# Second layer of a two-layer graph-attention kernel: denominators spread by small DMAs, both context halves transposed in one run, side results read a key tile later

## The chip, the cores and the metric

The kernel runs on one core of one Trainium2 chip. A core has five engines that work side by side, each through its own instructions in program order: TensorE (PE, matmul; PEld is its weight load), VectorE (DVE), ScalarE (ACT), GpSimd (POOL) and SyncE (SP, which here issues DMAs). The metric is the device time of one launch in microseconds (us), lower is better.

## What is computed

Two layers over 8 graphs of 2048 nodes with 256 features. The first layer is attention by chunks of keys under an adjacency mask, with a projection and a layer norm; the change does not touch it. The second layer, the one that matters here, is a graph attention with 4 heads of 64 features:

```python
h = relu(layernorm(x));  q = (h @ W).reshape(B, N, H, D)
e = e_src[:, :, None, :] + e_dst[:, None, :, :]
e = where(e >= 0, e, 0.2 * e);  e = where(adj > 0, e, -9e15)
h_prime = einsum('bijh,bjhd->bihd', softmax(e, axis=2), q)
x = x + elu(h_prime.reshape(B, N, H * D))
```

The kernel uses that exp of a leaky sum of two terms is the larger of two products, so a tile of the weights is one DVE instruction: the maximum of a row (`near`) and a per-key number (`far`), cut by the mask (`limit`). The softmax's denominators are summed beside the numerators and divided out at the end.

## The kernel before, in words

All of the second layer stands in `layers`, and its instruction order is written out by hand: what is recorded first on an engine runs first there.

**Passes and tiles.** There are 32 passes, one for each graph b and head h (`passes`), and each walks over 16 key tiles jt = 0..15 of 128 keys. The loop over `rounds` records for tile jt, in this order:

- `begun` for the tile two ahead: DVE makes `e` (L804, 128 x 2048; in tiles 0 and 15 as two halves). `e` has five buffers (`second_e`), so e of tile n + 5 can only be written when every reader of e of tile n is done. At tile 14 `begun` also records `nears` of the next pass (L795): ACT rewrites the one `near` buffer, after the last e of this pass has read it, and the next e waits for ACT.
- `weigh_rows` (L815): 8 matmuls of 32 x 512 into the two context banks `acc`, as 16 instructions.
- for the denominators, tiles are added in pairs m = 0..7 (tiles 2m, 2m + 1). On the even tile ACT scales e into `t` (L926, two halves); on the odd tile POOL adds the second e to it (L932, two halves). The sums of a pair are due two tiles after its odd tile (L826, into the bank `rest[:, 0]`, called `den`). Pairs 3 and 7 (`SINGLE`) go to PE without ACT and POOL.
- at tile 15, ACT copies the two banks `acc` to `cT` (L939) and `den` to `dT` (L948), and a generator `ending(k, cT, dT)` is put first in the list `aside`.
- `advance()` takes one step of the generators in `aside`. A step that ends with a bare `yield` has used the one side bank `rest[:, 1]` (`aux()`) and ends the call; one that ends with `yield True` lets the next generator have its step too.

**The end of a pass** (`ending`) is spread over the next pass's first tiles. Step by step: the load of `xh` (L842, SP; at tile 15); tile 0: four transposes (`flip`, L157) of `dT`, then the reciprocal and a maximum on DVE (L848, L849); tiles 1 and 2: four transposes of one context half each, and on DVE the product with the inverse denominators, `z` (L858); tiles 3 and 5: four ACT instructions for one half of the elu (L870 to L873); tiles 4 and 6: two POOL additions for that half (L875, L876); tile 7: the output DMA (L878, SP).

**The preparation of the next graph** (`preparation`, started in the first pass of every four, except for the last graph) shares the side bank. For four blocks of rows: ACT makes `h` (L145), PE transposes (`turn`, L157), ACT copies to `hT` (L165), twice, then 8 small matmuls (L622) and an ACT copy. Then reductions, two DMA hops, and a transpose of `er`. Then eight times: `sides` (L154, 32 instructions of 128*32 x 256) and the DVE product `qn` (L693) that reads its bank. A graph's four passes with a preparation in them are called a group below; there are seven groups, and then four plain passes (28 to 31) without one.

The functions that the change touches, with their callers:

## Time and profile before

| what | us |
|---|---|
| median of 3 runs (lowest, highest) | 4203.39 (4202.0, 4207.51) |
| the profiled execution's own time | 4210.55 |
| its span | 4208.7 |
| first instruction of L815 (second layer) | 2730.5 |
| last pass's `cT` copies begin | 4188.6 |
| mean granted TensorE clock | 0.994 |
| busy: PE / DVE / ACT / POOL | 4067.2 / 3159.1 / 2394.9 / 3263.0 |

The page gives shares over the whole span, and over two thirds of that is the first layer. The second layer's passes repeat: from pass 4 on, each group takes 183.6 us between the same copies of its passes, and each of the passes 28 to 30 takes 40.43 us. So one plain pass and one group are read in the timelines, and the rest is counted. An engine's idle time before an instruction, and what ended it, stand in brackets at the end of its line; "DVE e L804" there means that DVE's instruction of line 804 ended the wait.

### The profile page before, as it was taken

Reading aid. Unit: us, or ns where it says so; the run is one execution under the profiler, and the core shown is the slowest. Engines: PE = TensorE matmul, PEld = TensorE weight load, DVE = VectorE, ACT = ScalarE, POOL = GpSimd, SP = SyncE. Lnnn points to the kernel's source line nnn. Section 1 sums busy time; section 2 is a strip of 40 time slices with the busy share of each in tenths; the row PEclk is TensorE's granted clock in tenths of the full one; section 3 lists DMA queues with packets and bytes.
Section 4 is the critical chain, followed back from the end, with each engine's and each line's share of the span. In section 5 each row is a group of like instructions: output and inputs, shape, how many; then the busy total and the mean of one; then the engine's idle time right before and its main releaser. Section 6 shows DMA issues by size and latency. Waiting matters only on the chain. (4 is left out here: it accounts for less than half of the span.)

```text
span 4208.7 us, 85702 instructions
## 1 busy us (share of the span) xinstructions
PE 4067.2 (97%) x34998; PEld 1507.0 (36%) x34998; DVE 3159.1 (75%) x3526; ACT 2394.9 (57%) x3090; POOL 3263.0 (78%) x1735
## 2 busy tenths in 40 slices
PE   7999999999999999999999999889999999999998
PEld 3333333333333333333333333333333333333333
DVE  5786676666766677676677677588888988888897
ACT  5655565555565565555556556564555646555554
POOL 2577787888888888788788799777776877777687
PEclk9999999999999999999999999999999999999999
DMA  3221211112112112111211222221221222122121
GB/s 112 87 77 50 57 58 48 53 53 65 48 55 63 48 51 61 54 50 53 62 50 54 55 60 62 80 58 51 63 71 33 72 52 73 51 63 71 33 61 37
DMA packets 343235, 248.11 MB, mean 59 GB/s; under 512 B 225840, under 2 KB 293168, under 8 KB 342832
## 3 DMA queue, kind: packets, MB, share of 16 engines
q1 hardware_dynamic: 337648, 223.66, 19.6%
q0 software_dynamic: 5184, 18.88, 1.2%
q8 instruction: 277, 4.54, 0.4%
q14 instruction: 126, 1.03, 0.1%
HBM read 204.15 MB, written 36.18 MB: 57 GB/s over the span
## 5 line engine op out<-in xcount | busy, mean ns | idle before, releaser
L449 DVE SCALAR_TENSOR_TENSOR E<-big,limit 128x1024 f32<-128x1024 f32 x1024 | 1181.9, 1217 | 646.1 <-PE big L441 627.9
L742 POOL TENSOR_TENSOR add<-E 128x1024 f32<-128x1024 f32 x512 | 1203.7, 2374 | 496.1 <-PE both L461 472.7
L455 ACT ACTIVATE E<-E 128x1024 f32<-128x1024 f32 x1024 | 1055.7, 1057 | 687.8 <-DVE E L449 669.1
L804 DVE SCALAR_TENSOR_TENSOR e<-near,far,limit 128x2048 f32<-128x2048 f32 (+1 forms) x576 | 1183.0, 2107 | 94.3 <-issue 55.0
L932 POOL TENSOR_TENSOR t<-t,e 128x1024 f32<-128x1024 f32 x384 | 903.9, 2383 | 346.4 <-ACT t L926 196.0
L461 PE MATMUL both<-E,v 128*32 128x512 f32 x8192 | 993.9, 594 | 0.2
L815 PE MATMUL acc<-e,qn 128*32 128x512 f32 x8192 | 972.8, 595 | 5.3 <-DVE e L804 5.1
L441 PE MATMUL big<-qT,kT 64*128 64x512 f32 x4096 | 959.4, 606 | 14.6 <-DVE E L449 12.5
L441 PEld LDWEIGHTS big<-qT,kT 64*128 64x128 f32 x4096 | 366.2, 187 | 587.7 <-issue 419.8
L926 ACT ACTIVATE t<-e,quot 128x1024 f32<-128x1024 f32 x384 | 420.1, 1144 | 266.5 <-DVE e L804 153.1
L501 POOL TENSOR_TENSOR acc<-acc,c 128x1024 f32<-128x1024 f32 x224 | 531.2, 2371 | 4.6 <-DVE c L499 4.6
L461 PEld LDWEIGHTS both<-E,v 128*32 128x32 f32 x8192 | 294.3, 109 | 535.8 <-issue 396.7
L815 PEld LDWEIGHTS acc<-e,qn 128*32 128x32 f32 x8192 | 271.8, 110 | 496.0 <-issue 451.4
L499 DVE TENSOR_TENSOR c<-both,r 128x512 f32<-128x512 f32 x448 | 308.7, 690 | 42.3 <-PE both L461 10.6
L472 PE MATMUL big<-add,ones 128*32 128x512 f32 x2048 | 280.7, 601 | 13.9 <-POOL add L742 3.4
L826 PE MATMUL rest<-t,for_sums 128*32 128x512 f32 x1536 | 211.0, 594 | 22.2 <-DVE z L858 9.5
L479 ACT COPY s<-big 128x512 f32<-128x512 f32 x256 | 149.8, 585 | 71.1 <-PE big L472 70.8
L826 PE MATMUL rest<-e,for_sums 128*32 128x512 f32 x1024 | 141.0, 592 | 0.0
L145 ACT ACTIVATE h<-x,off,rstd 128x256 f32<-128x256 f32 x256 | 139.2, 593 | 0.0
L154 PE MATMUL rest<-w,hT 128*32 128x256 f32 x1952 | 122.1, 392 | 10.7 <-DVE qn L693 6.6
L795 ACT ACTIVATE near<-es,off_s 128x1024 f32<-128x1024 f32 x64 | 71.6, 1119 | 106.8 <-DVE e L804 95.8
L154 PE MATMUL big<-hT,wk 128*32 128x512 f32 x1024 | 124.2, 600 | 7.0 <-ACT hT L165 5.8
(133 smaller groups left out, 3031.3 us busy)
## 6 DMA issues: line engine op xcount, KB each, us to landing
r<-inv SPq DMA_DIRECT2D x1024, 64.0 KB
x<-in_x_dram SPq DMA_DIRECT2D x96, 512.0 KB
es<-er SPq DMA_DIRECT2D x64, 512.0 KB
adj_in<-in_adj_dram SPq DMA_DIRECT2D x32, 512.0 KB
x<-o POOLq DMA_DIRECT2D x32, 512.0 KB, 3.3
xh<-x SPq DMA_DIRECT2D x32, 512.0 KB
out_dram<-xh SPq DMA_DIRECT2D x32, 512.0 KB
x<-x SPq DMA_DIRECT2D x28, 512.0 KB
```

The lines of the kernel that those rows point to most:

```text
L441: nc.tensor.matmul(ps[:, hh, :], ks[kt // NT][own, hp, (kt % NT) * P : (kt % NT + 1) * P], qs[qb][own, hp, :], start=True, stop=True,)
L449: nc.vector.scalar_tensor_tensor(e, ps, -0.5, bcast(limit[:, qb, kt, :], 1, 2), ALU.max, ALU.min)
L455: nc.scalar.activation(e, e, AF.Exp, scale=0.25 * EDGE)
L461: nc.tensor.matmul(both[part][32 * h : 32 * h + 32, :], vs[kt // NT][:, kt % NT, mine], es[h // 2][:, h % 2, :], start=first, stop=not first,)
L499: nc.vector.tensor_tensor(to[:, part, :], both[part], r, ALU.mult)
L501: nc.gpsimd.tensor_tensor(acc, acc, to, ALU.add)
L742: nc.gpsimd.tensor_tensor(both, tiles[0][hp], tiles[1][hp], ALU.add)
L804: nc.vector.scalar_tensor_tensor(e[:, of, :], near[:, of, :], far[:, jt, h : h + 1], limit[:, of, jt, :], ALU.max, ALU.min,)
L815: nc.tensor.matmul(acc[part][32 * blk : 32 * blk + 32, :], qn[jt // NT][:, jt % NT, own], e[:, blk, :], start=(jt == 0), stop=(jt == NKT - 1),
L826: nc.tensor.matmul(den[32 * blk : 32 * blk + 32, :], for_sums[:, jt, :], blocks[blk], start=first, stop=last,)
L926: nc.scalar.activation(t, now[:, 2 * half : 2 * half + 2, :], AF.Copy, scale=quot[:, m, h : h + 1])
L932: nc.gpsimd.tensor_tensor(ts[half], ts[half], now[:, 2 * half : 2 * half + 2, :], ALU.add)
```

## The change

Only the second layer is changed.

- In `ending`, the four transposes of `dT` go. In their place SP issues four DMAs that spread the four rows of denominators over 128 partitions (16 bytes to each partition from each row); then the load of `xh` as four DMAs in place of one. Rows are now dealt to partitions as (block, partition, tile), so `cT` is copied from `acc` with a stride of four.
- Both context halves are transposed in one run of eight, into the side bank and into `den`'s bank, and the reciprocal, the maximum and both products follow each other on DVE.
- A list `unread` holds readers of side results. `aux()` and `advance()` call them first, so these are recorded one key tile later: the ACT copy to `hT`, the DVE products `qn`, and the reciprocal, maximum and products of the ending.
- With three steps fewer on the side bank, ending's later steps come two tiles earlier (elu halves on ACT at tiles 1 and 3, on POOL at tiles 2 and 4, output at tile 5), and so do the preparation's steps.
- The output goes out in four DMAs.

```diff
+    def read_all():
+        while unread:
+            unread.pop(0)()
+    def read_later(reader):
+        if rest:
+            unread.append(reader)
+        else:
+            reader()
     def aux(dtype=F32):
+        read_all()
         return rest[0][:, 1, :] if rest else pair(dtype)[:, 0, :]
...
-        nc.scalar.copy(
-            hT[:, :, two * 256 : (two + 1) * 256].rearrange("p c (t r) -> p c t r", t=2), ps
-        )
+        to = hT[:, :, two * 256 : (two + 1) * 256].rearrange("p c (t r) -> p c t r", t=2)
+        read_later(lambda: nc.scalar.copy(to, ps))
...
     def advance(all_of=True, mask_first=False):
+        read_all()
         moved = all_of and tick()
...
-                nc.vector.tensor_tensor(
-                    q[:, 2 * two : 2 * two + 2, :].rearrange("p t (h d) -> p (t h) d", h=H),
+                read_later(lambda to=q[:, 2 * two : 2 * two + 2, :], ps=ps, n=n: nc.vector.tensor_tensor(
+                    to.rearrange("p t (h d) -> p (t h) d", h=H),
...
     def ending(k, cT, dT):
...
-        nc.sync.dma_start(xs, column(x1[b], h))
+        r = small.tile([P, NQB, NT], F32, tag="inverse", name="inverse")
+        for blk in range(NQB):
+            nc.sync.dma_start(r[:, blk, :], dT[32 * blk : 32 * blk + 1, :].rearrange("o (p t) -> o p t", t=NT))
+        for blk, mine in enumerate(columns(x1[b], h)):
+            nc.sync.dma_start(xs[:, NT * blk : NT * blk + NT, :], mine)
         yield True
-        ps = aux().rearrange("p (c k) -> p c k", c=NT)
-        for c in range(NT):
-            flip(ps[:, c, :], dT[:, c * P : (c + 1) * P])
...
+        halves = [aux(), rest[0][:, 0, :]]
+        for part in range(2):
+            for t in range(NT):
+                flip(halves[part][:, t * P : (t + 1) * P], cT[:, part, t, :])
+        z = big.tile([P, NQB, NT, DH], F32, tag="c", name="z")
+        def product():
+            nc.vector.reciprocal(r, r)
+            nc.vector.tensor_reduce(inverse_most[:, k : k + 1], r, mybir.AxisListType.XY, ALU.max)
+            for part in range(2):
+                nc.vector.tensor_tensor(
+                    z[:, :, :, 32 * part : 32 * part + 32].rearrange("p b t d -> p t b d"),
+                    halves[part].rearrange("p (t b d) -> p t b d", t=NT, d=32),
+                    bcast(r.rearrange("p b t -> p t b"), 3, 32),
+                    ALU.mult,
+                )
+        read_later(product)
         yield
...
-        nc.sync.dma_start(column(out[b], h), xs)
+        for blk, mine in enumerate(columns(out[b], h)):
+            nc.sync.dma_start(mine, xs[:, NT * blk : NT * blk + NT, :])
...
-            cT = big.tile([P, 2, QB], F32, tag="hT", name="cT", bufs=1)
+            cT = big.tile([P, 2, NT, P], F32, tag="hT", name="cT", bufs=1)
             for part in range(2):
-                nc.scalar.copy(cT[:, part, :], acc[part])
+                nc.scalar.copy(cT[:, part, :, :], acc[part].rearrange("p (k t) -> p t k", t=NT))
```

More of the change, by code (lines that the diff above doesn't have):

```diff
@@ L100, in banks @@
         return [psum.tile([P, QB], F32, tag=f"both{k}", name=name) for k in range(2)]
+    unread = []
+    def read_all():
[6 more added lines that the diff above has]
+            reader()
     def aux(dtype=F32):
+        read_all()
         return rest[0][:, 1, :] if rest else pair(dtype)[:, 0, :]
@@ L697, in preparation @@
                     ALU.mult,
-                )
+                ))
                 if two == 1:
                     qn.append(q)
-                if blk == NQB - 1 and two == 1:
-                    shared[b] = qn, held, off_s, far, quot, flat
                 yield
+        shared[b] = qn, held, off_s, far, quot, flat
+        yield True
     def fill(qb):
@@ L832, in add_up_rows, with columns @@
             )
-    def column(to, h):
-        return to[:, h * DH : (h + 1) * DH].rearrange("(n p) d -> p n d", p=P)
+    def columns(to, h):
+        mine = to[:, h * DH : (h + 1) * DH].rearrange("(b p t) d -> b p t d", b=NQB, t=NT)
+        return [mine[blk] for blk in range(NQB)]
     def ending(k, cT, dT):
@@ L841, in ending @@
         xs = big.tile([P, NKT, DH], F32, tag="acc", name="xh")
-        nc.sync.dma_start(xs, column(x1[b], h))
-        yield True
-        ps = aux().rearrange("p (c k) -> p c k", c=NT)
-        for c in range(NT):
-            flip(ps[:, c, :], dT[:, c * P : (c + 1) * P])
-        r = small.tile([P, NT, NQB], F32, tag="inverse", name="inverse")
-        nc.vector.reciprocal(r, ps.rearrange("p c (b k) -> p c b k", k=32)[:, :, :, 0])
-        nc.vector.tensor_reduce(
-            inverse_most[:, k : k + 1], r.rearrange("p c b -> p (c b)"), mybir.AxisListType.X, ALU.max
-        )
@@ L852, in ending @@
-        yield
-        z = big.tile([P, NQB, NT, DH], F32, tag="c", name="z")
-        for part in range(2):
-            ps = aux().rearrange("p (t f) -> p t f", t=NT)
-            for t in range(NT):
-                flip(ps[:, t, :], cT[:, part, t * P : (t + 1) * P])
-            nc.vector.tensor_tensor(
-                z[:, :, :, 32 * part : 32 * part + 32].rearrange("p b t d -> p t b d"),
-                ps.rearrange("p t (b d) -> p t b d", d=32),
-                bcast(r, 3, 32),
-                ALU.mult,
-            )
-            yield
+        r = small.tile([P, NQB, NT], F32, tag="inverse", name="inverse")
```

## The prediction

> **What bounds the kernel now.** I read the shares first and then distrusted them: PE is 97% busy over the span, but most of that is the first layer. So I cut the second layer into its passes by the starts of the `cT` copies and asked for the busy time of two stretches, one group (passes 12 to 15) and one plain pass (28). Columns: stretch, its length, busy time of PE, PEld, DVE, ACT, POOL, clock, DMA.

> ```profile
> 3293.20:3476.80 183.60, 178.03 (x1752) 62.99 (x1748) 159.50 (x103) 100.86 (x137) 137.36 (x71) 1.00 0.22 60
> 4027.70:4068.10 40.40, 39.09 (x352) 13.95 (x348) 37.97 (x23) 21.90 (x26) 33.30 (x16) 1.00 0.20 52
> ```

> In the plain pass PE has 39.09 of 40.4 us and DVE 37.97, so two engines compete. The timeline of DVE through this pass decides it:

> ```profile
> 4027.19 7.00 DVE L804 SCALAR_TENSOR_TENSOR e<-near,far,limit 128x1024 f32<-128x1024 f32 x4 [2.39 <-issue]
> 4034.10 0.25 DVE L848 RECIPROCAL inverse<-rest 128x16 f32<-128x16 f32 x1
> 4034.38 0.17 DVE L849 TENSOR_REDUCE most<-inverse 128x1 f32<-128x16 f32 x1
> 4034.47 2.34 DVE L804 SCALAR_TENSOR_TENSOR e<-near,far,limit 128x2048 f32<-128x2048 f32 x1
> 4036.72 0.68 DVE L858 TENSOR_TENSOR z<-rest,inverse 128x512 f32<-128x512 f32 x1
> 4037.32 2.34 DVE L804 SCALAR_TENSOR_TENSOR e<-near,far,limit 128x2048 f32<-128x2048 f32 x1
> 4039.58 0.68 DVE L858 TENSOR_TENSOR z<-rest,inverse 128x512 f32<-128x512 f32 x1
> 4040.18 25.05 DVE L804 SCALAR_TENSOR_TENSOR e<-near,far,limit 128x2048 f32<-128x2048 f32 x12
> 4067.63 1.28 DVE L804 SCALAR_TENSOR_TENSOR e<-near,far,limit 128x1024 f32<-128x1024 f32 x1 [2.39 <-issue]
> ```

> Read from one first e to the next: 4067.63 - 4027.19 = 40.44, without any gap but the 2.39 in which ACT rewrites `near`. **A plain pass is one closed loop of DVE.** PE trails behind it (pass 28's first L815 starts at 4029.16, 1.97 after e0). A group is different: in its third pass PE is busy 51.3 of 52.5 us, with the eight side matmuls.

> Now the engines between DVE's products and DVE's later e, in the timelines of the same pass: ACT first, then POOL.

> ```profile
> 4034.22 2.19 ACT L926 ACTIVATE t<-e,quot 128x1024 f32<-128x1024 f32 x2 [1.59 <-DVE e L804]
> 4040.30 0.63 ACT L870 ACTIVATE low<-z 128x512 f32<-128x512 f32 x1 [3.89 <-DVE z L858]
> 4042.54 2.18 ACT L926 ACTIVATE t<-e,quot 128x1024 f32<-128x1024 f32 x2
> ```

> ```profile
> 4036.98 4.70 POOL L932 TENSOR_TENSOR t<-t,e 128x1024 f32<-128x1024 f32 x2 [0.16 <-DVE e L804]
> 4042.19 1.29 POOL L875 TENSOR_TENSOR z<-z,low 128x512 f32<-128x512 f32 x1 [0.51 <-ACT z L872]
> 4044.80 4.74 POOL L932 TENSOR_TENSOR t<-t,e 128x1024 f32<-128x1024 f32 x2
> ```

> POOL runs nearly without a pause from 4032.10 to 4066.2: pairs m0, m1, half 0 of the elu, m2, half 1, m4 to m6. m2 ends at 4049.5. It reads e of tile 5, whose buffer e of tile 10 takes at 4051.47: a slack of 1.95 us. That this slack can run out is seen in pass 12, where POOL has four more instructions (3.9 us, `roots`) ahead of the elu:

> ```profile
> 3318.49 13.77 DVE L804 SCALAR_TENSOR_TENSOR e<-near,far,limit 128x2048 f32<-128x2048 f32 x7 [1.40 <-POOL t L932]
> ```

> m2 ended at 3318.45 there, and e10 began 0.04 later.

> **The change, part by part.** Times of a pass are counted from its e0 (4027.19 is 0).

> *Transposes and the reciprocal's place.* A run of four costs PE 0.73 (4031.56 to 4032.15, and 0.14 of drain before it). Three runs become one of eight, about 1.32, so 0.87 is saved, and with it PE's waits for DVE between the runs (0.33, 0.55, 0.44 in a plain pass). DVE's own work stays: 0.38 + 2 x 0.60. In a plain pass PE is not what DVE waits for, so this is worth 0 there. Were PE the bound of all of a group, it would be worth 4 x 0.87 + 2.8 of waits = 6.3 us.

> *Small DMAs.* One operation of this kind is in the trace: `sum<-s`, 128 pieces of 64 bytes, from SP's issue to the waiting reciprocal 1.86 us. Issues of a row like it take 0.55 each, 0.61 apart. So four land 3 x 0.61 + 1.86 = 3.7 us after `dT`. `dT` ends at 2.82, they land at 6.5. The products are now recorded after e3, and DVE reaches them at 9.17: hidden, with 2.6 us over, by e1 to e3. When PE trails 1.7 us more (below), 1 us is left. Bounds for the four together: 1.9 (all beside each other) to 4 x 1.86 = 7.4 (one after the other); I take 3.7, which is what the row with the same work gives.

> [...]

> *The load of `xh` and the output in four.* SP issues 14 DMAs in a pass in place of 4, about 14 x 0.5 = 7 us of 40: free. But `xh` now stands behind the wait for `dT`, and the next `es` behind it. The packets of one load took 4053.3 to 4057.0; so `xh` is there at about 11 to 12, and ACT reads it at 12.6. `es` is needed 25 us later. I take 0; if the cover goes, up to 1 us.

> *The strided copy to `cT`*: L939 takes 0.585; no row shows a stride of four, so 0 to +0.6 for each. Behind it is `dT`, which waits 1.13 for PE anyway: 0.

> *The steps two tiles earlier.* **This is the term that decides.** Before, the elu's ACT instructions of half 0 were queued behind `t` of m1 (ACT at 7.03) and waited 3.89 for z with nothing but m2 behind them. Now they are recorded at tile 1, ahead of m1. ACT works in order, so m1's `t` waits for the products:
> - products start at 9.17 and end at 10.82 (before, z1 ended at 13.07);
> - elu half 0 on ACT, 10.86 to 13.1 (2.24 by the rows 4040.30 to 4042.54); then `t` of m1 13.1 to 15.3, six us later than before;
> - POOL: m0 ends at 9.6 to 11.3; half 0 can start at 12.75 and ends at 15.4; m1 (4.7) ends at 20.1; half 1, now ahead of m2, at 22.7; m2 at 27.4, where it was 22.3;
> - DVE: e10 would start at 24.28, and waits for m2's e buffer until 27.43. From there nothing is late: 5 x 2.26 + 2.4 + 2.4 to the next e0, 43.6.

> So a plain pass takes **+3.15 us**. PE waits too, for m1's sums (17.1 to 20.1) and m2's, and ends its pass 47.2, 3.65 after the next e0 rather than 1.97. In a lasting row of such passes it has 3.8 us of slack again at m1, so DVE's loop holds.

> *The groups.* I follow the same queue order through the four passes, less exactly.
> - First: the 3.9 us of `roots` now stand before half 0, m2 ends at 28.2 to 29.8 where it was 25.73: +2.4 to +4.1. ACT's blocks behind the `hT` copies (4.97 at 3321.04) go; instead the next transposes into the same bank wait for the later copy. +3.
> - Second: DVE waited 2.66 for the `dT` transposes, since PE trails by 7; now it waits about 1.7 to 3 for the small DMAs behind that late `dT`, and the 3.15 comes on top. The maximum over `er` waits for a copy that is queued behind m2's `t`. +3 (1 to 5).
> - Third and fourth: the side matmuls now begin at tile 1, and the first must wait until z0 is read (10.2), 2 to 3 us of PE; against it stand PE's 0.87 and 1.2 each. The reads of `qn` a tile later turn DVE's waits (8.1 us in this group) into none, but PE is the bound there, so that is worth little. The fourth pass starts without left-over side matmuls and takes 43.6 where it took 44.3. +1 for both.

> A group: **+7**, from +2 to +11.

> *The end.* The products of the last pass come 3.7 + 1.65 = 5.35 after `dT` where it was 4.4: +1; the last output DMA is a quarter of the size but issued up to 1.3 later: 0. Start of the layer: 0.

> **Sum.** 7 groups x 7 + 4 plain x 3.15 + 1 = 49 + 12.6 + 1 = +62.6. The profiled execution would take 4210.55 + 62.6 = 4273; it lies 7.2 above the median, so the prediction is **4266**.

> **Rivals.**
> 1. *Faster: PE is the bound, and ACT's order does not bind.* For it: PE's 178.03 of 183.6. It needs POOL's m2 to end within 24.28, so 3.1 us earlier than I count. Then plain passes stay at 40.44 and groups gain 6.3: -44, so 4160. Against it: ACT's idle 3.89 before L870 shows that the queue really waits there.
> 2. *No change*: the chain costs its 3.15 in plain passes, and the groups win back 2 each: 12.6 + 1 - 14 = 0, 4203.
> 3. *Slower still: the four DMAs do not overlap.* Landing 7.4 after `dT`, at 4.5 + 7.4 = 11.9 in the lasting state, the products start 2.7 later and all behind them: +2.7 in 31 passes, +84 on top, 4350. It decides from a landing of 4.7 us on.

> **How the numbers follow.** The forecast 0.76, rival 1 0.09, rival 2 0.05, rival 3 0.10. The forecast's own range: groups at +2 give 14 + 13.6 = +28, at +11 +91: 4231 to 4294. For 8 in 10 I reach a little to both sides, to half the chain's price (4212) and to an extra 0.5 us a pass from the DMAs (4310). Faster by over 0.2% (8.4 us, about what a measurement of this kernel can tell from no change) 0.09, within 0.05, slower 0.86.

> **What would show it.** In the changed profile's plain pass: DVE's product block follows e3 without a gap (right about the DMAs) or after a wait for a DMA (rival 3); an idle stretch of some 3 us before e10, ended by POOL's t; 43.6 from e0 to e0; ACT's elu half 0 ahead of m1's `t`; PE waiting for POOL at m1 and m2. If e10 has no gap and the pass still takes 40.44, the deciding step is wrong. If the group takes less than 183.6, rival 1 is right.

## The result, and the profile after

The changed kernel takes **4350.34 us** (median of 4 runs, 4345.67 to 4351.85); the runs of the kernel before beside it have a median of 4203.40. The ratio is 1.0344, with a 95% interval of 1.0331 to 1.0357: 147 us slower, where I had forecast 63 and a range up to 4310. The direction was right, the size too small. The profiled execution took 4345.67, its span is 4343.9.

Where the difference lies, from the first e (L819, which was L804) of each pass to the next, in the two profiled executions:

| part | before | after | difference | predicted |
|---|---|---|---|---|
| first e of the layer | 2729.1 | 2720.1 | -9.0 | 0 |
| first group | 196.3 | 210.8 | +14.5 | +7 |
| six later groups, mean of one | 183.6 | 202.7 | +19.07 each, +114.4 | +7 each, +42 |
| of these: first pass | 43.0 | 47.2 to 49.5 | +5.7 | +3 |
| second pass | 45.6 | 50.0 to 52.4 | +5.7 | +3 |
| third and fourth pass | 95.0 | 101.8 to 102.8 | +7.7 | +1 |
| passes 28 to 30, each | 40.44 | 43.5 | +3.1 each, +9.3 | +3.15 each |
| last pass, from its first e to the end | 60.2 | 66.1 | +5.9 | +4.15 |

The sum is +135, the difference of the spans. The two profiled executions stand 7.2 above and 4.7 below the medians of their runs, which makes it 147. The earlier start fits the granted clock: ahead of the layer's first e, before had 30.7 us of half clock in all (13.65 of them from 2709.3 on, just ahead of it), after 13.7, and half of that difference is 8.5.

The plain pass came as predicted. This is DVE's timeline through pass 29 of the changed kernel (start, length, operation, how many; in brackets the idle time before it and what ended it):

```profile
4190.62 9.25 DVE L819 SCALAR_TENSOR_TENSOR e<-near,far,limit 128x1024 f32<-128x1024 f32 x5 [2.39 <-issue]
4199.79 0.24 DVE L872 RECIPROCAL inverse<-inverse 128x16 f32<-128x16 f32 x1
...
4200.16 1.28 DVE L875 TENSOR_TENSOR z<-rest,inverse 128x512 f32<-128x512 f32 x2
4201.35 9.12 DVE L819 SCALAR_TENSOR_TENSOR e<-near,far,limit 128x2048 f32<-128x2048 f32 x4
4210.70 4.61 DVE L819 SCALAR_TENSOR_TENSOR e<-near,far,limit 128x2048 f32<-128x2048 f32 x2 [0.23 <-POOL t L952]
4217.95 13.77 DVE L819 SCALAR_TENSOR_TENSOR e<-near,far,limit 128x2048 f32<-128x2048 f32 x7 [2.63 <-POOL t L952]
4234.11 1.28 DVE L819 SCALAR_TENSOR_TENSOR e<-near,far,limit 128x1024 f32<-128x1024 f32 x1 [2.39 <-issue]
```

The reciprocal follows e3 without a wait, 9.17 after e0, so the small DMAs are there. The second gap, 2.63, stands before e10, at 27.33 after e0 (predicted 27.43). Here are the ACT and POOL instructions of the same pass that lead to it, in two views:

```profile
4201.47 0.63 ACT L889 ACTIVATE low<-z 128x512 f32<-128x512 f32 x1 [3.81 <-DVE z L875]
...
4203.71 2.18 ACT L946 ACTIVATE t<-e,quot 128x1024 f32<-128x1024 f32 x2
```

```profile
4205.97 4.70 POOL L952 TENSOR_TENSOR t<-t,e 128x1024 f32<-128x1024 f32 x2
...
4213.22 14.22 POOL L952 TENSOR_TENSOR t<-t,e 128x1024 f32<-128x1024 f32 x6
```

ACT reaches m1's `t` at 13.09 after e0 (predicted 13.1), behind the elu; POOL starts m1 at 15.35 (predicted 15.4), and begins m2 at 22.6 (predicted 22.7).

The groups did not come as predicted. This is a part of DVE's timeline in the third pass of one (pass 14, 3435.19 to 3494.52):

```profile
3449.23 0.69 DVE L708 TENSOR_TENSOR qn<-rest,share 128x512 f32<-128x512 f32 x1 [0.97 <-PE rest L169]
...
3455.79 0.69 DVE L708 TENSOR_TENSOR qn<-rest,share 128x512 f32<-128x512 f32 x1 [3.61 <-PE rest L841]
...
3464.58 0.69 DVE L708 TENSOR_TENSOR qn<-rest,share 128x512 f32<-128x512 f32 x1 [2.99 <-PE rest L841]
...
3469.91 0.69 DVE L708 TENSOR_TENSOR qn<-rest,share 128x512 f32<-128x512 f32 x1 [2.37 <-PE rest L841]
```

L841 (L826 before) is the sums of denominators. They go to the *other* half of the tile `rest`, and `qn` reads nothing of theirs; yet the read waits for them. Over the whole second layer, these are rows of the waits (engine, line, what it waited for: us, times, longest), after and then before:

```profile
DVE qn L708 <- PE rest L841: 84.5, 28, 4.2
...
ACT hT L181 <- PE rest L841: 61.1, 27, 4.9
...
PEld rest L169 <- DVE qn L708: 53.4, 44, 1.8
...
DVE ends L649 <- ACT er L644: 31.7, 7, 7.0
```

```profile
ACT hT L165 <- PE rest L157: 88.1, 45, 5.0
...
DVE qn L693 <- PE rest L154: 58.5, 51, 2.6
...
PE rest L826 <- DVE z L858: 9.5, 24, 0.4
...
DVE ends L634 <- ACT er L629: 6.6, 6, 1.1
PEld rest L154 <- DVE qn L693: 8.3, 28, 0.3
```

Before, `qn` waited only for its own matmuls, and the next side matmuls hardly waited for `qn` (8.3 us). After, the 28 waits for sums take 84.5 us, and PE in turn waits for `qn`. ACT's copies to `hT`, the other late reader, wait for sums too (61.1 us), where before they waited for their own transposes. The same coupling was in the trace of before the other way round, in the row `rest L826 <- DVE z`: sums into `den` waited for a read of the side half. I had not read that row.

One more thing is new in the groups. Each row here is a stretch, its length, busy time of PE, PEld, DVE, ACT, POOL, then PEclk, DMA share and GB/s; pass 14 is the second:

```profile
3336.29:3538.01 201.72, 180.92 (x1736) 60.10 (x1732) 159.68 (x102) 101.24 (x137) 137.11 (x71) 0.97 0.21 54
3435.19:3494.52 59.33, 53.22 (x604) 19.87 (x596) 43.34 (x30) 22.30 (x29) 33.25 (x16) 0.97 0.14 37
...
3446.64:3450.05 3.41, 3.41 (x36) 1.52 (x29) 2.44 (x3) 3.38 (x6) 2.05 (x2) 0.50 0.72 246
```

For 3.41 us the granted clock was 0.50. In the second layer up to its last pass there are 78.5 us of half clock, where before had 3.4.

### The profile page after: what moved, and what is told of

Its sections match the earlier page's. It is cut to its first block, busy times and chain, and to the rows that moved or that the text cites. A ratio compares the mean times of both kernels' runs of the same rounds, so it can differ in the third digit from the quotient of the medians.

```text
span 4343.9 us, 86071 instructions
## 1 busy us (share of the span) xinstructions
PE 4080.8 (94%) x34870; PEld 1469.7 (34%) x34870; DVE 3160.4 (73%) x3526; ACT 2396.6 (55%) x3090; POOL 3261.6 (75%) x1735
## 4 chain that ended last, share of the span: by engine, by line
PE 71%; POOL 9%; ACT 7%; DVE 5%; issue 4%; DMA 3%; SPq 1%; ACTq 0%; POOLq 0%; DVEq 0%
PE big L456 17%; PE both L476 15%; PE acc L830 14%; PE big L169 8%; PE big L487 6%; PE rest L841 5%; POOL add L757 3%; PE rest L169 3%; POOL t L952 2%; POOL acc L516 2%; ACT E L470 2%; ACT t L946 1%; DVE e L819 1%; DMA inverse<-dT 1%; PE big L172 1%
## 5 line engine op out<-in xcount | busy, mean ns | idle before, releaser
L819 DVE SCALAR_TENSOR_TENSOR e<-near,far,limit 128x2048 f32<-128x2048 f32 (+1 forms) x576 | 1179.9, 2105 | 153.7 <-POOL t L952 79.2
L830 PE MATMUL acc<-e,qn 128*32 128x512 f32 x8192 | 1032.9, 606 | 15.2 <-DVE e L819 15.1
L514 DVE TENSOR_TENSOR c<-both,r 128x512 f32<-128x512 f32 x448 | 308.4, 689 | 43.4 <-PE both L476 13.7
L841 PE MATMUL rest<-t,for_sums 128*32 128x512 f32 x1536 | 254.3, 603 | 34.5 <-POOL t L952 32.9
L841 PE MATMUL rest<-e,for_sums 128*32 128x512 f32 x1024 | 170.3, 593 | 0.0
L169 PE MATMUL big<-hT,wq 128*32 128x512 f32 x1024 | 124.4, 600 | 1.1 <-ACT hT L181 0.7
```

Of the source, the lines that this page charges most:

```text
L169: nc.tensor.matmul(to[j : j + 32], lhsT[:, j : j + 32], rhs, start=start, stop=stop)
L819: nc.vector.scalar_tensor_tensor(e[:, of, :], near[:, of, :], far[:, jt, h : h + 1], limit[:, of, jt, :], ALU.max, ALU.min,)
L830: nc.tensor.matmul(acc[part][32 * blk : 32 * blk + 32, :], qn[jt // NT][:, jt % NT, own], e[:, blk, :], start=(jt == 0), stop=(jt == NKT - 1),
L841: nc.tensor.matmul(den[32 * blk : 32 * blk + 32, :], for_sums[:, jt, :], blocks[blk], start=first, stop=last,)
```

## The experiments

After the result I held three causes for the loss in the groups, to be told apart: (a) the earlier steps, as in the plain pass; (b) late readers that wait by whole tile, so that the side half and `den` block each other; (c) PE's standing, which brings the half clock. The rival from the prediction, DMAs that don't overlap, would show as DVE's waits for `inverse<-dT`. Letters A and B within an expectation are defined there. Each ratio is against the kernel before on the same chip; "group" is the mean of the six later ones.

### The side area as two tiles

```diff
-    rest.append(psum.tile([P, 2, QB], F32, tag="rest", name="rest"))
+    for name in ("den", "rest"):
+        rest.append(psum.tile([P, QB], F32, tag=name, name=name))
```

`aux()` then gives `rest[1]`, and `den` is `rest[0]`; nothing else changes.

> The changed kernel with the two halves of the side area as two tiles (den and rest) in place of one tile of two banks. In the changed kernel's third pass DVE's qn reads wait for the denominator sums (L841) of their own tile, which write the other half. Theory A (a late reader of one half waits for the last writer of the whole tile): those waits go, the third pass of a group falls from 59.3 to about 54 us between first e's, hT copies in the first two passes end earlier, the group falls from 201.7 to 192-196, the time from 4350 to 4285-4315; plain passes stay at 43.5. Rival B (the loss is the single side bank itself: the next writer must wait for a reader that comes a tile later, whatever tile it lies in): third pass stays within 1.5 us, time 4340-4355.

Measured: 4286.87, ratio 1.0198 (1.0181 to 1.0215): 63.5 us less than the changed kernel. A group takes 194.3 (202.7), its third pass 54.60 or 52.92 (59.33 or 57.64); a plain pass stays at 43.49. What `qn` waits for, in us and times:

```profile
  PE rest L169: 69.1, 54
```

The waits for the sums are gone, those of the copies to `hT` too, and what is left is for its own matmuls. Cause (b) is shown, for less than half of the loss.

### The elu's steps two tiles later

```diff
         read_later(product)
         yield
+        for _ in range(2):
+            yield True
```

This puts the elu and the output back to their old tiles, and leaves the preparation's steps early.

> The changed kernel with the elu steps of the ending put off by two key tiles, so ACT has the t of pair m1 ahead of the elu again, as before the change. Theory A (ACT's order delays m1, POOL's m2 and so DVE's e10): the gap before e10 in a plain pass goes from 2.6 to 0, the plain pass from 43.5 to 40.4, the four plain passes give 12 us; groups fall by 3 to 8 each through their first, second and fourth passes; time 4270-4315. Rival B (something else, as the DMAs, makes the plain pass longer): plain stays within 0.5 of 43.5, time 4340-4355.

Measured: 4279.66, ratio 1.0178 (1.0161 to 1.0195): 70.7 less than the changed kernel. The plain pass on DVE:

```profile
4145.16 1.28 DVE L875 TENSOR_TENSOR z<-rest,inverse 128x512 f32<-128x512 f32 x2
4146.36 27.31 DVE L819 SCALAR_TENSOR_TENSOR e<-near,far,limit 128x2048 f32<-128x2048 f32 x13
4176.06 2.48 DVE L819 SCALAR_TENSOR_TENSOR e<-near,far,limit 128x1024 f32<-128x1024 f32 x2 [2.39 <-issue]
```

Thirteen e follow the products without a gap, and the pass takes 40.43 (4135.63 to 4176.06), as before. So the earlier place of the elu in ACT's and POOL's order is the whole of the plain pass's loss, as predicted. A group takes 193.9: the fourth pass falls to 40.43, the third stays at 57.6 to 59.3, and `qn` still waits 83.0 us for the sums.

### Both together

The two edits above.

> Both edits together. Theory A: they add up, since one acts on the third passes and the other on the plain ones: 4205-4280, plain pass 40.4. Rival B: no more than 10 us below the changed kernel.

Measured: 4211.26, ratio 1.0019 (1.0010 to 1.0029). A group takes 183.4. The gains of the two edits alone add up to 134.2 us, together they give 139.1: they are separate causes, and together nearly the whole of the loss against the kernel before. (Against the kernel before with its own tile split, below, 25 us stay.)

### hT and qn read at once

```diff
-        read_later(lambda: nc.scalar.copy(to, ps))
+        nc.scalar.copy(to, ps)
```

The same for `qn`, with the tile left as one and the steps early; the ending's products are still read late.

> The changed kernel with the ACT copies to hT and the DVE products qn recorded at once again, as before the change; only the ending's reads stay a key tile later. Theory A (reading these a tile later is what makes groups so much slower, through the side tile): the third pass falls from 59.3 to 51-54, the group from 201.7 to 186-192, time 4250-4290, with plain passes still 43.5. Rival B (the groups lose through the order of the ending's steps and the clock alone): the third pass stays above 57, time over 4325.

Measured: 4293.87, ratio 1.0214 (1.0197 to 1.0231). That is 56.5 less than the changed kernel, but the third pass, 57.46, stayed far above what I had expected, and so did the group (195.1). The waits for the sums are gone and others stand in their place: `qn` waits 85.5 us for its own matmuls, which begin at tile 1 and have no lead there. The early preparation steps are a cost of their own, which this experiment could not part from the rest.

### PE kept at work ahead of the side matmuls

```diff
+        if rest and b:
+            for k in range(3):
+                for blk in range(NQB):
+                    nc.tensor.matmul(
+                        acc[k % 2][32 * blk : 32 * blk + 24, :], wa[:, 0, 2 * H :], now[:, blk, :], start=False, stop=False
+                    )
```

Matmuls with weights of zero, put ahead of each later graph's first side matmul, while PE would stand.

> The changed kernel with 12 matmuls by zero weights (the unused columns of wa, added into the context banks, which they leave as they are) ahead of each graph's first side matmul, where PE stood still for 2.8 us in the third pass and the granted clock then fell to a half for 3.4 us. Nothing of the computation changes. Theory A (a stand of 2.8 us costs the half clock, and that costs the pass 1.7 us): the 2.8 us are filled, no half clock follows, the third pass takes 57.6 in place of 59.3 in nearly every group; the time falls by 8 to 13 us. Rival B (the half clock after it falls on time that PE has to spare): third pass unchanged within 0.3, time 4342-4355; rival C (the extra matmuls only add to PE's work): up to 2.6 us more in each group, time 4355-4370.

Measured: 4336.65, ratio 1.0314 (1.0297 to 1.0332): 13.7 less, with runs (4335.88 to 4337.86) that lie clear of the changed kernel's. PE's timeline at the place, in the changed kernel and then with the matmuls of zeros (L704):

```profile
3441.33 1.92 PE L830 MATMUL acc<-e,qn 128*32 128x512 f32 x16
3446.05 3.13 PE L169 MATMUL rest<-w,hT 128*32 128x256 f32 x32 [2.80 <-DVE z L875]
```

```profile
3443.72 2.76 PE L704 MATMUL acc<-e,wa 128*24 128x512 f32 x24
3446.70 1.93 PE L169 MATMUL rest<-w,hT 128*32 128x256 f32 x32 [0.23 <-DVE z L881]
```

In the first, PE stands 2.80 and the next side matmuls take 3.13 for 32; in the second it stands 0.23 and they take 1.93. The later groups' third pass takes 57.64 to 57.77 in all six, and the half clock from 78.5 to 41.0 us. More work for PE made the kernel faster: cause (c) is shown. What the filled stands give directly is the 8.3 us of the six later third passes; the rest of the 13.7 came mostly in the first passes, where nothing was filled and less half clock fell. The third pass with 3.41 us of half clock and without, 59.33 and 57.64, prices them at 1.69, about half of 3.41.

### The tile split in the kernel before

The edit of the first experiment, made in the kernel before.

> The kernel before, with its side area as two tiles of one bank each in place of one tile of two. Theory A (whole-tile dependency, which before cost PE only the waits of the sums for z and qn): plain passes stay at 40.44, since DVE closes their loop; third passes, which PE bounds, gain 0.3 to 1 us; time 4193-4204. Rival B (the dependency matters as much as in the changed kernel, 7 us a group): 4145-4160.

Measured: 4185.82, ratio 0.9954 (0.9938 to 0.9971): faster than both kernels, and by more than I had expected. A group takes 181.5 (183.6): 0.77 less in the second pass, 1.34 less in the fourth. The coupling already cost the kernel before, so the change without it is best held against this kernel.

### Split, steps later, and read at once

The edits of the first, second and fourth experiment.

> The changed kernel with all three edits: two tiles, the elu steps two tiles later, and hT and qn read at once. What is left of the change is the small DMAs, the transposes in one run with the products together, and the preparation two tiles earlier. Theory A: plain passes 40.4; DVE waits for the side matmuls again, so the third pass stays near 53-57 as with the immediate reads alone; time 4200-4235, no better than the two edits without it (4211). Rival B (late readers are the loss even with two tiles): 4150-4190.

Measured: 4212.44, ratio 1.0017 (1.0007 to 1.0027): no better than with late reads. The third pass takes 56.86, against 52.92 in "both together", and the second 43.3 against 45.3.

### The side bank kept a tile longer

To "both together":

```diff
-        for _ in range(2):
-            yield True
+        yield
+        yield True
```

The ending keeps the bank at tile 1, so the side matmuls start later and PE need not stand for z.

> The changed kernel with two tiles, the elu steps two tiles later, and in addition nothing of the preparation on the side bank at tile 1 (the ending keeps the bank until its products are recorded). Theory A: PE no longer stands 2.8 us in front of the first side matmul and no half clock follows it; the third pass falls from 52.9 to 49.5-51.5, groups to 179-182, time 4185-4200, below the kernel before. Rival B (the wait only moves to another place): third pass 52.5 or more, time 4205-4215.

Measured: 4207.96, ratio 1.0010 (1.0000 to 1.0020); the expectation was missed. The half clock fell to 6.8 us, and the third pass to 52.06 without any. But the second pass takes 46.2 to 47.2 in place of 45.3, and a group 184.3 in place of 183.4. Taking away the half clock was worth little here, since the steps that moved made other waits.

### Only the DMAs, the one run of transposes and the strided copy

Split, read at once, and:

```diff
         read_later(product)
-        yield
+        for _ in range(3):
+            yield
```

The ending keeps the side bank for three tiles as it used to, so the elu, the output and the preparation stand at their old tiles. Of the change, the four DMAs, the load and output in four, the strided copy, the run of eight and the late products are left.

> The small DMAs, the strided copy and the one run of transposes with the products together, and nothing else of the change: two tiles, hT and qn read at once, and the ending keeps the side bank for three tiles as before, so every later step stands at its old tile. To be compared with the kernel before with two tiles (4186). Theory A (these edits were never the cost; they save PE 0.87 and the waits between the runs where PE is the bound): plain passes 40.4, third passes 49-50.6, time 4165-4190. Rival B (the wait for the small DMAs, 2.6 us in the second passes, or SP's longer queue costs more than the transposes did): second passes over 46, time 4192-4215.

Measured: **4184.09** (4179.86 to 4185.89), ratio 0.9947 (0.9930 to 0.9963), faster than both kernels and the fastest of the study. A group takes 180.9, 0.6 below the kernel before with its tile split, and the plain pass 40.43. Against that kernel (0.9954, with overlapping intervals) there is no difference that these runs can tell. So the edits in the first part of the change's name cost nothing, and bring next to nothing: the gain is the split.

Beside "split, steps later, and read at once" it differs only in the three tiles for which the bank is kept, and is 28.4 us faster: with reads at once, the preparation's early start costs that much (third pass 56.86 against 50.57).

### Only the late readers, in the kernel before

`hT` and `qn` through `read_later`, and `shared` set one step later, as the change has it; one tile, and everything else as before.

> The kernel before with one edit of the change alone: hT and qn are read a key tile later, its ending and its one side tile unchanged. Theory A (late readers wait for the sums of the same tile, and the next writer waits for them): third passes 52-54.5 with qn ended by L826, groups 2-6 us longer, time 4215-4250, plain passes 40.44. Rival B (late reads cost only together with the earlier steps): 4196-4208.

Measured: 4261.08, ratio 1.0131 (1.0114 to 1.0148): about 55 us slower, more than expected. A group takes 191.5, but not where I had put the loss: the third pass *fell* to 48.35, the second rose to 49.92 and the fourth to 48.38. Rows of the waits that name it:

```profile
DVE inverse L863 <- PE rest L172: 44.4, 14, 6.0
...
DVE qn L708 <- PE rest L841: 32.9, 16, 3.2
...
DVE ends L649 <- ACT er L644: 25.4, 7, 5.1
...
DVE qn L708 <- ACT dT L963: 23.1, 6, 3.8
```

The second and the fourth are readers of one half that wait for work on the other (sums, and the copy of `den`). The third is the chain to `er`, which stands behind the late copies of `hT`. The first, the reciprocal's wait for its transposes, was 22.8 before; in each later second pass it grew from 2.66 to 4.7, and `ends` from 1.1 to 3.4, which together is that pass's loss of 4.3.

### Late readers with the split and the old tiles

The fastest kernel, with `hT` and `qn` read a tile later.

> The core edits as above with two tiles and every step at its old tile, but with hT and qn read a key tile later. Theory A (with two tiles a late read costs little: it takes DVE's waits away and gives PE a wait of its own): within 8 us of the same kernel with immediate reads, third passes 49-51.5. Rival B (the single side bank makes a late read dear by itself): third passes 53 or more, time 4205-4225.

Measured: 4203.55, ratio 0.9995 (0.9986 to 1.0005): 19.5 above the fastest kernel, where I had expected no more than 8. A group takes 183.4: the third pass gains 3.4, the second loses 2.2 to 3.9 and the fourth about 2; the wait of `ends` for `er` is 25.1 us (4.8 in the fastest kernel), and the half clock 23.9. Late reads cost something even without the coupling, but only at the old tiles. With the split and the elu at its old tiles, the four kernels are: read at once, 4184.09 with the preparation at its old tiles and 4212.44 with it early; read late, 4203.55 and 4211.26. So late reads and the early start do not add: each costs 19 to 28 us alone, and with late reads, as the change has them, the early start costs 7.7 us.

## Why the prediction was right in direction and wrong in size

- **Transposes worth 0 in plain passes, small DMAs hidden, strided copy, `xh` and output 0: right.** The small DMAs landed 4.15 after the end of `dT` where the reciprocal shows it (pass 13: `dT` ended at 3391.12, the reciprocal began at 3395.27), 4.0 to 4.8 in the six later second passes, against 3.7 predicted. So they overlap: four times 1.86 would be 7.4. In these passes DVE waits 2.4 to 3.2 for them; I had 1.7 to 3. In the plain passes little was left over: `dT` ends 4.43 after e0 in pass 29 and the products start 4.74 later, so the predicted reserve of 1 us was nearly used up. The copy to `cT` takes 0.58, as without the stride. In the experiment with only the DMAs, the run of eight and the strided copy they cost nothing that can be told (4184.09, against 4185.82 for the kernel before with its tile split).
- **Steps two tiles earlier: right to 0.1 us**, by its own chain (m1's `t` at 13.09, m2 begun at 22.6, e10 at 27.33, pass 43.5), and shown by the second experiment: with the steps back, the gap before e10 and the 3.1 us of each plain pass are gone.
- **The groups: wrong, the step that failed.** I had put +7, from +2 to +11; it was +17.6 to +20.6 in the later ones. The term that was farthest off is the "+1 for both" of the third and fourth pass: the fourth came as predicted (43.6), and the third took 8.4 more. Two sentences carry it. "The reads of `qn` a tile later turn DVE's waits (8.1 us in this group) into none": they turned into waits of 84.5 us over the layer, since here a reader waited for the last writer of its whole tile (28 waits, none of them left with two tiles) and the next writer for that reader (PEld for `qn`, 53.4 us). The split tile gives back 8.4 per group, 4.7 of them in the third pass. And "+1 for both" left out that the side matmuls, begun at tile 1, run without a lead. I did count the 2 to 3 us for which PE stands for z (2.80), but not the half clock that follows: about 1.7 for each 3.41 us of it, 8.3 us over the six later third passes.
- The first and second passes each had +3, and got +5.7. In the later first passes DVE's wait for POOL's `t` grew from 1.4 to 4.7 (mean of the six), which is the predicted chain; what I had not counted is `near`, which ACT rewrites late there, so that the next e0 waits 4.1 to 5.8, where before it waited 3.5 for POOL. In the second passes the predicted 3.15 did not occur, since no e there waits for POOL. In its place `ends` waits 4.1 (1.1), the chain behind the late copy of `hT`, which I had named and priced too low (31.7 us in 7 waits over the layer, before 6.6), and `far` waits 2.1 for PE (before 0).
- **The end**: from `dT` to the products' end 5.7, where before it was 4.4: +1.3 against +1. The last pass also has its 3.1, and PE, later behind DVE than I had carried on to the end, 1.5 more.
- **Rivals.** The measured time is nearly that of rival 3, but by coincidence: its mechanism did not occur. In plain passes the products follow e3 without a gap, or with 0.06. Rival 1 is out, since DVE does wait for POOL's m2, and rival 2, since the groups lost 19 each where it had them win 2.
- What stays open: why the first pass varies between 47.2 and 49.5 from group to group, and how far each of the coupling, the late reads and the half clock makes `near`, `ends` and `far` late. The experiments move all three at once there.

## What to carry to other kernels

Before a reader is moved later, list who writes *anything* in its tile between the old place and the new: here the waits counted by tile, with 84.5 us of `qn` for sums in the other bank of its tile, and none once the two banks were two tiles. Where a stall is priced, look at what the engine does next to it: here a stand of 2.80 us on PE brought 1.69 more by the half clock that followed it (59.33 against 57.64). And when a change frees steps that others follow, price the move of those others as an edit of its own, in the kernel that it is made in; here it cost 28 us with side results read at once, and 8 with them read late.

## What the runs showed of the hardware that I had not expected

The half clock came with quite short stands of PE. In the six later groups of the changed kernel, a stand of 2.27 us in the second pass was followed by half clock four times of six, one of 2.80 in the third pass five times of six, and the longest stand of the first pass (2.98 to 4.53) had it in all six, five times for 6.83 us in place of 3.41. In the first group a stand of 3.55 brought none.

```profile
3443.23:3446.63 3.40, 0.60 (x16) 0.41 (x16) 3.37 (x6) 0.60 (x1) 2.58 (x2) 1.00 0.86 222
3446.64:3450.05 3.41, 3.41 (x36) 1.52 (x29) 2.44 (x3) 3.38 (x6) 2.05 (x2) 0.50 0.72 246
...
4054.22:4057.62 3.40, 1.41 (x28) 0.89 (x32) 3.37 (x6) 1.40 (x3) 1.75 (x1) 1.00 0.93 219
4057.63:4061.04 3.41, 3.41 (x56) 1.53 (x52) 3.41 (x3) 3.41 (x5) 2.88 (x3) 1.00 0.61 211
```

In the trace of the kernel before, its layer cut in the same steps from the start of half clock at 2709.31, there is one more start, at 2746.85, 11 steps behind. In the stretch ahead of that start PE stood for 1.75 us; the one from 2736.61 on, with 1.93, had no half clock behind it. The ends of matmuls are modelled in the profile, so these lengths are no sharper than that. In the changed kernel the stand of 2.80 was followed by half clock in pass 14 and not in pass 26, and these passes took 59.33 and 57.64.
